# A graph network layer: three and two fetched sets of edges by turns instead of two, and two and one instead of one

## The chip, the cores and the metric

The kernel runs on one core of a Trainium2 chip. The metric is the device time of one execution in microseconds (us); lower is better.

## The reference

50,000 nodes with 160 features (64 scalars `s`, 32 vectors `v` of three) and 1,650,000 edges sorted by destination. Each edge brings the features of its source node, multiplied with four numbers of its own; the products are summed by destination, go through linear maps, and the result is added and normalised:

```python
ss, vv = (s[src], v[src])
e0 = sh[:, 0:1]; e1 = sh[:, 1:4]
dot = jnp.einsum('eui,ei->eu', vv, e1)
out0 = C0 * (ss * e0 @ W1 + dot * INV3 @ W2)
p3 = (ss @ W3)[:, :, None] * e1[:, None, :] * INV3
p4 = jnp.einsum('eui,uw->ewi', vv * e0[:, :, None], W4) * INV3
p5 = jnp.einsum('eui,uw->ewi', jnp.cross(vv, e1[:, None, :]), W5) * INV6
out1 = C1 * (p3 + p4 + p5)
m = jnp.concatenate([out0, out1.reshape(-1, 3 * MUL1)], axis=1)
m_agg = jax.ops.segment_sum(m, dst, num_segments=n)
...
return x + jax.nn.relu(h)          # h: m_agg through Ws and Wv
# outside: _layernorm(x + that, axis=-1)
```

## The kernel before

All maps are linear in the source's features, so the kernel sums first: for each destination it sums (four numbers of the edge) x (160 features of its source), and multiplies with one combined weight matrix afterwards.

Edges stand in sets of 128, called units in the code. Six sets make a group (`G`), whose destinations lie within 32 slots; two groups make a pair (`PG`), ten pairs (`per`) a chunk of 120 sets. For each set PE multiplies a 128x128 operand `ha` (slot times the four numbers, made by VectorE at L474 and L477 one pair ahead) with the 128x160 features of the sources (L502). After a pair VectorE transposes the sums (L518) and adds them into a ring of node sums in SBUF (L527). When 128 nodes are complete, `do_block` (PE, L822) multiplies with the weights, two such blocks at a time go through the normalisation (`norm1` on VectorE at L185 to L190, the root on ScalarE at L195, `norm3` on VectorE at L199 to L201), and SyncE sends the result (L920).

The features of the sources are the gathers. Most sets come by one indirect DMA that POOL issues (`gather`, L459) into `xg`, a pool of four buffers of a pair each, so POOL can be ahead of PE by up to four pairs. The others are fetched by ScalarE and SyncE (`Fetcher`, L351 to L391): for each of 128 edges the engine issues a DMA of one row of 640 bytes (L376) at an address from a register; 32 registers at a time are loaded from the list that VectorE made (`list_rows`, L403 and L404; load at L372). PE waits for the set's own semaphore. `deal` spreads the rows of a chunk evenly over ten pairs, from the fourth pair of the chunk before (`FBEGIN`) on; the place of a set in its chunk is chosen so that it is used four pairs (`FWAIT`) after its last row was issued. `BY_SCALAR` and `BY_SYNC` are the sets in a chunk; each pool has one buffer more. Fetching covers all chunks but the first two and the last.

SyncE's queue also issues all other transfers in program order. For a pair p: raw edge data of the chunk after next (`load`, L270 and L276, three pairs before a chunk begins); the residual rows `xt` of a pair of blocks (L765); the nodes' own rows and shares for the ring (`ask_own`, L798, five pairs before they are due, used by `set_own` at L807 two pairs before); the results.

Besides, the edges without self loops are packed. A "pack" takes 128 rows of 1,185 edges (SyncE reads them, L596 to L600), converts them on ScalarE (L604 to L606, L624), compacts them on VectorE (L625 to L690) and stores them row by row from SyncE into a table in DRAM (`store`, L739, two DMAs a row), which later chunks read instead of the raw edges. There are 11 packs; each pack's steps are spread over the pairs until it is due, its stores are 17 of them with one step between each two, and the next pack's conversion (L604) reuses the buffer that the stores read. Packs are due about every nine chunks; the first, which is needed soonest, has its stores within about one chunk.

All engines but POOL keep the order in which the program issues their work.

Of the kernel before, what the change touches and what calls it, by code (L numbers as in the profile page):

```python
# [39 lines left out]
F32 = mybir.dt.float32  # L40
I32 = mybir.dt.int32
# [3 lines left out]
ALU = mybir.AluOpType  # L45
AX = mybir.AxisListType
ET = mybir.EngineType
# [3 lines left out]
P = 128  # L51
MUL0, MUL1 = 64, 32
D = MUL0 + 3 * MUL1
# [10 lines left out]
W = 32  # L64
# [3 lines left out]
PG = 2  # L68
# [9 lines left out]
KM = WS - 1  # L78
REST = 15
LEAD = 3  # L80
BY_SCALAR, BY_SYNC = 2, 1
FBEGIN, FWAIT = 4, 4

def plan(n_nodes, n_edges):

    nblk = 125
    assert n_nodes % nblk == 0
    assert W == FB
    nb = n_nodes // nblk
    again = 9  # L90

    per_unit = P * n_nodes / n_edges
    group = max(g for g in range(1, 17)
                if g == 1 or (g + 0.2) * per_unit + 1 + 5 * math.sqrt(g * per_unit * per_unit / P) <= W)
    head = math.ceil(min(HEAD, n_edges / (group * P)) / SG) * SG
    eh = head * group * P
    row = group * P * 3 // 2 + math.floor(per_unit * group * 3 / 2 * (1 - n_nodes / n_edges))
    assert row * n_nodes / n_edges + 5 * math.sqrt(row * n_nodes / n_edges / 16) < KM

    far = math.ceil(6 * math.sqrt(n_edges) / 2 * n_nodes / n_edges) + 2  # L100
    rows = math.ceil((n_edges - eh) / row) + 2
# [7 lines left out]
def tile_gnn_resnorm(ctx: ExitStack, tc: tile.TileContext, x, src, dst, attr, W1, W2, W3, W4, W5, Ws, Wv, out, n_edges):  # L109
    nc = tc.nc  # L110
    N = x.shape[0]
    NBLK, NB, GA, G, NU, NG, L, NH, NR, FAR = plan(N, n_edges)
# [107 lines left out]
    NSC = math.ceil(NG / SG)  # L220
# [12 lines left out]
    with tc.tile_pool(name="once", bufs=1) as once, tc.tile_pool(name="raw", bufs=2) as rawp, \  # L233
# [8 lines left out]
        spotp, ownp, listp, heldp, scalarp, syncp = (  # L242
            later_pools.enter_context(tc.tile_pool(name=name, bufs=bufs))
            for name, bufs in (("spot", 3), ("own", 2), ("list", 2), ("held", 1),
                               ("scalar", BY_SCALAR + 1), ("sync", BY_SYNC + 1)))
        extremes = once.tile([P, 2, NSC], F32, name="extremes")
        count_ = once.tile([1, SG], F32, name="count")
        nc.gpsimd.iota(count_, pattern=[[1, SG]], base=0, channel_multiplier=0, allow_small_or_imprecise_dtypes=True)
# [8 lines left out]
        per = SG // PG  # L257
# [92 lines left out]

        class Fetcher:  # L351

            def __init__(self, engine, et, pool, n, place):
                self.engine, self.et, self.pool, self.n = engine, et, pool, n
                self.rows, self.turn, self.left, self.asked = deque(), 0, 0, []
                self.landed = [tc.alloc_semaphore(f"{pool.name}{i}") for i in range(4 * (n + 1))]
                self.spots = [math.ceil((FBEGIN + per * (i + 1) / n + FWAIT - per) * PG * G) + place for i in range(n)]
                assert all(0 <= at < per * PG * G for at in self.spots)

            def prepare(self, s, line, at, u):  # L360

# [19 lines left out]

                self.rows.extend(partial(one, q, e) for q in range(P // W) for e in range(W))

            def begin(self, wanted):
                assert len(self.rows) == wanted * self.n * P
                self.left = len(self.rows)

            def deal(self, gone):
                keep = math.floor(P * self.n * (1 - gone))
                while self.left > keep:  # L390
                    self.rows.popleft()()  # L391
                    self.left -= 1

        fetchers = [Fetcher(*f) for f in ((nc.scalar, ET.Activation, scalarp, BY_SCALAR, 2), (nc.sync, ET.SP, syncp, BY_SYNC, 8)) if f[3]]
        wanted = [(f, at) for f in fetchers for at in f.spots]
        assert len({at for _, at in wanted}) == len(wanted)

        def list_rows(s, u0, ef):

            line = listp.tile([P, len(wanted), W], I32, name="line")  # L400
            held = heldp.tile([P, len(wanted), W], F32, name="held")
            for i, (f, at) in enumerate(wanted):
                nc.vector.tensor_scalar(held[:, i], ef[:, 0, (u0 + at) % NK], 0.0, float(N - 1), op0=ALU.max, op1=ALU.min)  # L403
            nc.vector.tensor_scalar(line, held, float(4 * D), None, op0=ALU.mult)  # L404
            for i, (f, at) in enumerate(wanted):
                f.prepare(s, line[:, i], at, u0 + at)

# [436 lines left out]
        spots = once.tile([1, 2 * npacks * RP], I32, name="spots")  # L844
# [10 lines left out]
        counts = once.tile([P, 2, npacks], F32, name="counts")  # L855
# [9 lines left out]
        def after_pair(p, f, *args):  # L865
            later.setdefault(p, []).append((f, args))
# [135 lines left out]
        for p, (s, g, ng) in enumerate(pairs):  # L1002
            if (p + LEAD) % per == 0 and (p + LEAD) // per + 1 < NSC or not p:
                ahead_ = (p + LEAD) // per + 1
                end = reach(ahead_)
                assert end <= 0 or rows_stored[0] == NR or end <= row_start(rows_stored[0])[0][0]
                raws[ahead_] = load(ahead_)
            if p % per == 0 and s + 1 < NSC:
                after_pair(p + 1, do_cast, s + 1)
                after_pair(p + 2, do_place, s + 1)  # L1010
                if s + 2 == NSC:
                    after_pair(p + 4, examine_all)
                    after_pair(p + 6, read_flags)
            rows = gather(s, placed[s], (g - s * SG) * G, ng * G)
            for j, ps in enumerate(group_sums(p, rows, has.pop(p))):
                if j == 1 and turning:
                    turn_sums(*turning)
                    turning = None
                if j == 3 and p + 1 < len(pairs):
                    s1, g1, ng1 = pairs[p + 1]  # L1020
                    has[p + 1] = spread(placed[s1], (g1 - s1 * SG) * G, ng1 * G)
                work(1.0)
                if p % per == FBEGIN and not j:
                    begun_at = p
                    for f in fetchers:
                        f.begin(0 < s < NSC - 2)
                for f in fetchers:
                    if f.left:
                        f.deal((p - begun_at + (j + 1) / (ng * G)) / per)
                if packs and p >= START:  # L1030
                    when = p + (j + 1) / (ng * G)
                    todo = math.ceil(len(packs[0]) * min(1, (when - began) / max(1, due[0] - began)))
                    for step in packs[0][done:todo]:
                        if step:
                            step()
                    done = max(done, todo)
                    if done == len(packs[0]):
# [37 lines left out]
    with tc.tile_pool(name="up", bufs=1) as up, tc.tile_pool(name="us", bufs=2) as us, tc.For_i(0, once_more, 1):  # L1075
# [18 lines left out]
        for s in range(nseg):  # L1094
# [7 lines left out]
            for c in range(CB):  # L1102
# [3 lines left out]
                at = us.tile([PB, 2, SEG], F32, name="at")  # L1106
# [5 lines left out]
        f = up.tile([PB, CB], F32, name="f")  # L1112
# [12 lines left out]
    with tc.tile_pool(name="edges2", bufs=2) as ep, tc.tile_pool(name="ops2", bufs=2) as op, \  # L1125
            tc.tile_pool(name="node2", bufs=1) as np_, tc.tile_pool(name="psA2", bufs=2, space=PSUM) as psA, \
            tc.tile_pool(name="psF2", bufs=1, space=PSUM) as psF:
        with tc.For_i(0, blocks, 1) as b:
# [35 lines left out]
            for h in range(2):  # L1164
# [3 lines left out]
                at = np_.tile([D // 2, NK, NBLK], F32, name=f"ac{h}")  # L1168
# [3 lines left out]
            i = 0  # L1172
# [44 lines left out]
```

## Time and profile before

| | |
|---|---|
| Median of 3 runs | 15449.47 us (15443.1 to 15450.64) |
| Profiled execution | 15440.23 us, its span 15438.1 us |
| Granted TensorE clock, mean | 0.578 |
| Indirect gathers on POOL (L459) | 12,216 |
| Rows issued by ScalarE, by SyncE (L376) | 26,112 and 13,056 |

Rows of the profile name engine, line, operation and tiles; "x" is a count. A group's last columns are busy us, the mean ns of one, and the idle time before its instructions with what ended it; "issue" is time in which an engine waited for nothing that the profile shows. Rows of the view of waits read "who <- whom: us in total, times, longest us". Timeline rows are start and duration in us. ACTq and SPq are DMAs issued from ScalarE's and SyncE's queues; issuing is not counted as busy time. In the view of one line, three numbers with slashes are the shortest, median and longest duration in ns, followed by the first and last start in us.

### The profile page before, as it was taken

To read this page: it belongs to the slowest core of one execution; us is meant where nothing else is said; L and a number is where in the kernel's file an instruction comes from. 1 tells how busy PE (TensorE), PEld (TensorE's weight loads), DVE (VectorE), ACT (ScalarE), POOL (GpSimd) and SP (SyncE) were. 2 spreads that over 40 slices of the span, in tenths; PEclk is the share of its full clock that TensorE was granted. 3 is DMA by queue.
4 is the path that set the end of the run, shared out by engine and by line. 5 is a ranking of instruction groups with operands and counts; after the bars stand their busy time and mean duration, and the time that the engine had idled before them with its cause. 6 is when DMAs were issued, how large, how long until landed. Compare 5 with 4: busy or idle time off the path is not lost.

```text
span 15438.1 us, 175175 instructions
## 1 busy us (share of the span) xinstructions
PE 10171.0 (66%) x28971; PEld 6746.8 (44%) x28972; DVE 7652.8 (50%) x12634; ACT 171.5 (1%) x273; POOL 11585.0 (75%) x12229
## 2 busy tenths in 40 slices
PE   3466666666666666666666666666666666666666
PEld 3344444444444444444444444444444444444444
DVE  8465355435635553563455355435634553554333
ACT  0000000000000000000000000000000000000000
POOL 7677777777777777777777777777777777777777
PEclk6655555555555555555555555555555555555555
DMA  3333333333333333333333333333333333333332
GB/s 83 87 85 93 93 81 83 98 86 85 91 93 83 84 95 89 84 84 97 85 85 91 91 82 85 96 89 83 83 100 86 82 87 93 81 86 85 85 82 75
DMA packets 909328, 1346.94 MB, mean 87 GB/s; under 512 B 292862, under 2 KB 683298, under 8 KB 905526
## 3 DMA queue, kind: packets, MB, share of 16 engines
q0 software_dynamic: 586368, 1001.52, 25.4%
q1 hardware_dynamic: 268330, 316.48, 6.6%
q10 hardware_dynamic: 53488, 17.70, 0.6%
q14 instruction: 911, 7.46, 0.2%
q8 instruction: 231, 3.78, 0.1%
HBM read 1263.28 MB, written 71.42 MB: 86 GB/s over the span
## 4 chain that ended last, share of the span: by engine, by line
POOL 51%; issue 21%; DMA 19%; PE 4%; DVE 1%; SPq 0%; POOLq 0%; DVEq 0%
POOL xg L459 51%; DMA xg<-in_x,si 18%; PE ps L502 3%; DMA selves<-mine 1%; PE phb L822 0%; DVE ha L477 0%; SPq L739 0%; DVE prow L688 0%; DVE ring L527 0%; SPq L376 0%; DMA xt<-in_x 0%; DVE sums L518 0%; DVE hot L474 0%; DVE ring L813 0%; DVE xr L809 0%
## 5 line engine op out<-in xcount | busy, mean ns | idle before, releaser
L459 POOL DMA_INDIRECT xg<-in_x,si x12216 | 11581.5, 948 | 3831.6 <-issue 3491.8
L502 PE MATMUL ps<-xg,ha 128*128 128x160 f32 x24432 | 9418.3, 500 | 5253.2 <-DMA xg<-in_x,si 4659.5
L502 PEld LDWEIGHTS ps<-xg,ha 128*128 128x128 f32 x24432 | 5765.7, 292 | 8675.4 <-DMA xg<-in_x,si 7382.9
L518 DVE STREAM_TRANSPOSE sums<-ps 128x320 f32<-128x320 f32 x1044 | 536.1, 513 | 6766.0 <-PE ps L502 6736.7
L477 DVE TENSOR_TENSOR ha<-hot,pk 128x1536 f32<-128x1536 f32 x1044 | 1830.4, 1753 | 35.8
L822 PE MATMUL phb<-BWk,ring 128*128 128x160 f32 (+1 forms) x3910 | 1250.3, 417 | 0.0
L822 PEld LDWEIGHTS phb<-BWk,ring 128*128 128x128 f32 (+1 forms) x3910 | 1020.3, 294 | 0.0
L527 DVE TENSOR_TENSOR ring<-ring,sums 128x160 f32 x2087 | 684.5, 328 | 338.0 <-issue 202.3
L474 DVE TENSOR_TENSOR hot<-bank,rel 128x384 f32<-128x384 f32 x1044 | 573.1, 549 | 69.9 <-DMA xt<-in_x 68.1
L688 DVE COPY_PREDICATED prow<-marks,prow 128x2370 f32<-128x2370 int32 (+5 forms) x198 | 548.6, 2770 | 1.1
L813 DVE STREAM_TRANSPOSE ring<-xr 128x1280 f32<-128x1280 f32 x188 | 468.7, 2493 | 6.5
L688 DVE COPY_PREDICATED pra<-marks,pra 128x1580 f32<-128x1580 int32 (+5 forms) x198 | 377.1, 1905 | 0.0
L809 DVE TENSOR_TENSOR xr<-xr,bank 128x1280 f32<-128x1280 f32 x188 | 278.9, 1483 | 6.6 <-DVE bank L808 0.2
L185 DVE SCALAR_TENSOR_TENSOR y<-phb,xt 128x320 f32<-128x320 f32 x196 | 95.5, 487 | 256.7 <-PE phb L822 256.0
L195 ACT ACTIVATE rstd<-mv,eps_t 128x2 f32<-128x2 f32 x196 | 58.0, 296 | 14013.9 <-DVE mv L190 13216.5
L524 DVE TENSOR_TENSOR ring<-ring 128x196 f32<-128x196 f32 (+20 forms) x485 | 149.3, 374 | 1.8
L502 PE MATMUL ps<-xscalar,ha 128*128 128x160 f32 x408 | 146.9, 462 | 0.0
L201 DVE TENSOR_SCALAR o<-y,mv,rstd 128x160 f32<-128x160 f32 x391 | 130.8, 376 | 7.5
L685 DVE COPY_PREDICATED_SCALAR hit<-marks,none 128x395 int32 (+5 forms) x198 | 129.8, 655 | 7.0
L772 DVE MEMSET ring<- 128x1280 f32 (+1 forms) x98 | 119.3, 1218 | 22.6 <-issue 22.6
L189 DVE BATCH_NORM_STATS2 st<-y 128x6 f32<-128x160 f32 x391 | 121.6, 311 | 6.7
L686 DVE COPY_PREDICATED hit<-marks,pri 128x395 int32<-128x395 int32 (+5 forms) x198 | 118.2, 597 | 6.8
(353 smaller groups left out, 2187.4 us busy)
## 6 DMA issues: line engine op xcount, KB each, us to landing
xscalar<-in_x ACTq DMA_DIRECT2D x26112, 0.6 KB
xsync<-in_x SPq DMA_DIRECT2D x13056, 0.6 KB
xg<-in_x,si POOLq DMA_INDIRECT x12216
xr<-in_x SPq DMA_DIRECT2D x187, 640.0 KB
r<-edges SPq DMA_DIRECT2D x100, 384.0 KB
edges<-prow SPq DMA_DIRECT2D x1330, 27.8 KB
xt<-in_x SPq DMA_DIRECT2D x195, 160.0 KB
out<-o SPq DMA_DIRECT2D x195, 160.0 KB
```

Source lines behind the costliest of these rows:

```text
L201: nc.vector.tensor_scalar(o[:n, i], y[:n, i], mv[:n, i, 0:1], rstd[:n, i:i + 1], op0=ALU.subtract, op1=ALU.mult)
L459: nc.gpsimd.indirect_dma_start(out=xg[:, j, :], out_offset=None, in_=x, in_offset=bass.IndirectOffsetOnAxis(ap=placed[0][:, u + j:u + j + ...
L474: idle[:] = [nc.vector.tensor_tensor(hot[:, :n], slotsP[:, 0:W].unsqueeze(1).to_broadcast([P, n, W]), rel[:, u:u + n].unsqueeze(2).to_broa ...
L477: nc.vector.tensor_tensor(ha[:, :n], hot[:, :n].unsqueeze(2).to_broadcast([P, n, NK, W]), pk[:, :, u:u + n].rearrange("p k u -> p u k").un ...
L502: mm = nc.tensor.matmul(ps[:, j // G, :], ha[:, j].rearrange("p k w -> p (k w)"), xr, start=j % G == 0, stop=j % G == G - 1)
L518: nc.vector.transpose(at[:, :ng], ps[:, :ng].rearrange("p g (b f) -> p g b f", f=FB))
L524: nc.vector.tensor_tensor(ring[k][:, b, :past], ring[k][:, b, :past], ring[k - 1][:, b, S:S + past], op=ALU.add)
L527: nc.vector.tensor_tensor(here, here, at[:, i], op=ALU.add)
L688: nc.vector.copy_predicated(what[:n, a:e], mi[:, r].unsqueeze(2).to_broadcast([n, e - a, what.shape[2]]), what[:n, a + d:e + d])
L809: nc.vector.tensor_tensor(xr[:, :nq], xr[:, :nq], sumP[:, :nq].unsqueeze(2).to_broadcast([P, nq, D]), op=ALU.mult)
L813: nc.vector.transpose(ring[k][:, :, c0:c0 + nq * W].rearrange("p b (w q) -> p q b w", q=nq), xr[:, :nq].rearrange("p q (b f) -> p q b f", ...
L822: wrote("misc", nc.tensor.matmul(ph[:nb], ring[k][:, i, c0:c0 + nb], BWk[:, i, :], start=i == 0, stop=i == ND - 1))
```

## The change

The number of fetched sets becomes a function of the chunk. ScalarE fetches three sets for chunk 6, two for chunk 7, and so on by turns; SyncE two for chunk 8, one for chunk 9, and so on. Chunks 2 to 5 have no fetched set from ScalarE and chunks 2 to 7 none from SyncE. The places of the sets in a chunk follow from the count by the same rule as before, both pools have a buffer more, and a chunk with nothing to fetch makes no list.

```diff
-BY_SCALAR, BY_SYNC = 2, 1
+BY_SCALAR, SCALAR_FIRST = (3, 2), 6
+BY_SYNC, SYNC_FIRST = (2, 1), 8
...
-                               ("scalar", BY_SCALAR + 1), ("sync", BY_SYNC + 1)))
+                               ("scalar", max(BY_SCALAR) + 1), ("sync", max(BY_SYNC) + 1)))
...
-                self.spots = [math.ceil((FBEGIN + per * (i + 1) / n + FWAIT - per) * PG * G) + place for i in range(n)]
-                assert all(0 <= at < per * PG * G for at in self.spots)
+            def spots(self, s):
+                n = self.counts[s % len(self.counts)] if self.first <= s < NSC - 1 else 0
+                ats = [math.ceil((FBEGIN + per * (i + 1) / n + FWAIT - per) * PG * G) + self.place for i in range(n)]
+                assert all(0 <= at < per * PG * G for at in ats)
+                return ats
...
-            def begin(self, wanted):
-                assert len(self.rows) == wanted * self.n * P
-                self.left = len(self.rows)
+            def begin(self, s):
+                assert not self.left and len(self.rows) == len(self.spots(s + 1)) * P
+                self.all = self.left = len(self.rows)
...
-                keep = math.floor(P * self.n * (1 - gone))
+                keep = math.floor(self.all * (1 - gone))
...
+        MOST = max(BY_SCALAR) + max(BY_SYNC)
+        fetchers = [Fetcher(nc.scalar, ET.Activation, scalarp, BY_SCALAR, SCALAR_FIRST, 2),
+                    Fetcher(nc.sync, ET.SP, syncp, BY_SYNC, SYNC_FIRST, 8)]
...
+            wanted = [(f, at) for f in fetchers for at in f.spots(s)]
+            assert len({at for _, at in wanted}) == len(wanted)
+            if not wanted:
+                return
+            line = listp.tile([P, MOST, W], I32, name="line")
...
-                        f.begin(0 < s < NSC - 2)
+                        f.begin(s)
```

More of the change, by code (lines that the diff above doesn't have):

```diff
@@ L351, in tile_gnn_resnorm, with __init__ @@
         class Fetcher:
[L353 to L356, printed above, removed]
-                self.spots = [math.ceil((FBEGIN + per * (i + 1) / n + FWAIT - per) * PG * G) + place for i in range(n)]
-                assert all(0 <= at < per * PG * G for at in self.spots)
+            def __init__(self, engine, et, pool, counts, first, place):
+                self.engine, self.et, self.pool, self.counts, self.first, self.place = engine, et, pool, counts, first, place
+                self.rows, self.turn, self.all, self.left, self.asked = deque(), 0, 0, 0, []
+                self.landed = [tc.alloc_semaphore(f"{pool.name}{i}") for i in range(4 * (max(counts) + 1))]
+            def spots(self, s):
[3 more added lines that the diff above has]
+                return ats
             def prepare(self, s, line, at, u):
@@ L392, in deal @@
                     self.left -= 1
-        fetchers = [Fetcher(*f) for f in ((nc.scalar, ET.Activation, scalarp, BY_SCALAR, 2), (nc.sync, ET.SP, syncp, BY_SYNC, 8)) if f[3]]
-        wanted = [(f, at) for f in fetchers for at in f.spots]
-        assert len({at for _, at in wanted}) == len(wanted)
+        MOST = max(BY_SCALAR) + max(BY_SYNC)
+        fetchers = [Fetcher(nc.scalar, ET.Activation, scalarp, BY_SCALAR, SCALAR_FIRST, 2),
+                    Fetcher(nc.sync, ET.SP, syncp, BY_SYNC, SYNC_FIRST, 8)]
         def list_rows(s, u0, ef):
-            line = listp.tile([P, len(wanted), W], I32, name="line")
-            held = heldp.tile([P, len(wanted), W], F32, name="held")
+            wanted = [(f, at) for f in fetchers for at in f.spots(s)]
[3 more added lines that the diff above has]
+            line = listp.tile([P, MOST, W], I32, name="line")
+            held = heldp.tile([P, MOST, W], F32, name="held")
             for i, (f, at) in enumerate(wanted):
                 nc.vector.tensor_scalar(held[:, i], ef[:, 0, (u0 + at) % NK], 0.0, float(N - 1), op0=ALU.max, op1=ALU.min)
-            nc.vector.tensor_scalar(line, held, float(4 * D), None, op0=ALU.mult)
+            nc.vector.tensor_scalar(line[:, :len(wanted)], held[:, :len(wanted)], float(4 * D), None, op0=ALU.mult)
             for i, (f, at) in enumerate(wanted):
```

## The prediction

> **What bounds the kernel now.** I read the page first, then POOL's waits over the whole span and without its first 700 us, then the timeline of POOL.
>
> ```profile
> span 15438.1 us, 175175 instructions
> POOL 51%; issue 21%; DMA 19%; PE 4%; DVE 1%; SPq 0%; POOLq 0%; DVEq 0%
> L459 POOL DMA_INDIRECT xg<-in_x,si x12216 | 11581.5, 948 | 3831.6 <-issue 3491.8
> xscalar<-in_x ACTq DMA_DIRECT2D x26112, 0.6 KB
> xsync<-in_x SPq DMA_DIRECT2D x13056, 0.6 KB
> q0 software_dynamic: 586368, 1001.52, 25.4%
> q10 hardware_dynamic: 53488, 17.70, 0.6%
> ```
> ```profile
> POOL xg L459 <- issue: 3491.8, 11413, 2.0
> POOL xg L459 <- PE ps L502: 185.1, 437, 33.7
> ```
> ```profile
> POOL xg L459 <- PE ps L502: 133.2, 423, 1.1
> ```
> ```profile
> 8008.34 0.95 POOL L459 DMA_INDIRECT xg<-in_x,si  x1 [0.30 <-issue]
> 8009.60 0.95 POOL L459 DMA_INDIRECT xg<-in_x,si  x1 [0.30 <-issue]
> 8010.85 0.95 POOL L459 DMA_INDIRECT xg<-in_x,si  x1 [0.30 <-issue]
> ```
>
> POOL issues one gather of 128 edges after another: 0.95 us of work and 0.30 us before the next, a pitch of 1.25 us. 12,216 gathers at that pitch are 15,270 us of the 15,438. The chain says the same: POOL and issue hold 72%, and "DMA" on it is the landing of POOL's gathers. POOL almost never waits for anyone: the fourth view (waits from 700 us to 15,400 us) has no wait for PE over 1.1 us, the whole span has one of 33.7 us. So time is (number of gathers) x 1.25 us, plus what stalls POOL, and the only stall is in the first 700 us.
>
> The other sets of 128 edges, 26,112 / 128 = 204 and 13,056 / 128 = 102, come as single rows from ScalarE's and SyncE's queues. PE's matmuls are the same whichever way a set comes:
>
> ```profile
> PE 10171.0 (66%) x28971; PEld 6746.8 (44%) x28972; DVE 7652.8 (50%) x12634; ACT 171.5 (1%) x273; POOL 11585.0 (75%) x12229
> ```
>
> PE is busy 66% and DVE 50%, so neither takes POOL's place when POOL does one per cent less.
>
> **The change part by part.** *Fewer gathers.* There are 12,216 + 306 = 12,522 sets, 120 to a chunk, so 105 chunks (0 to 104); 2 to 103 are now served by the queues. After: ScalarE serves chunks 6 to 103, 49 with three sets and 49 with two, 245 sets; SyncE serves 8 to 103, 48 with two and 48 with one, 144 sets. Together 389 against 306, so 83 gathers leave POOL: 83 x 1.25 = 104 us. On the path, since POOL waits for nothing in the steady part.
>
> *ScalarE's issue time.* Its rows in two chunks of the middle:
>
> ```profile
> 7949.86 34.49 ACTq L376 DMA_DIRECT2D xscalar<-in_x  x90
> 8007.05 0.30 ACT L195 ACTIVATE rstd<-mv,eps_t 128x2 f32<-128x2 f32 x1 [87.63 <-DVE mv L190]
> 8007.12 65.88 ACTq L376 DMA_DIRECT2D xscalar<-in_x  x128
> 8082.40 0.29 ACT L195 ACTIVATE rstd<-mv,eps_t 128x2 f32<-128x2 f32 x1 [75.05 <-DVE mv L190]
> 8082.47 37.69 ACTq L376 DMA_DIRECT2D xscalar<-in_x  x90
> ```
>
> A row costs 34.49 / 90 = 0.38 to 37.69 / 90 = 0.42 us with the loading of its addresses; the 128 in 65.88 us hold a wait besides. Three sets are 384 x 0.40 = 154 us, two are 102 us. A chunk will last 115 to 117 gathers, 144 to 146 us. ScalarE falls some 10 us behind in a chunk of three and regains 44 us in one of two: 256 us of 290. Its rows have four pairs of groups (58 us) between the end of their issue and their use, and the normalisation's root (L195) waits for DVE today, so ScalarE comes to it early. I cost this at nothing; the cover is the 58 us for rows, and for the root the one pair (14.6 us) until VectorE uses it.
>
> *SyncE's issue time, in quiet chunks and while the row table is stored.* Quiet, and in a stretch in which a pack's rows are stored (L739):
>
> ```profile
> 8066.86 13.45 SPq L376 DMA_DIRECT2D xsync<-in_x  x33
> ```
> ```profile
> 8574.45 0.29 SPq L739 DMA_DIRECT2D edges<-prow  x1
> ...
> 8585.31 0.22 SPq L739 DMA_DIRECT2D selves<-mine  x1
> 8585.62 5.74 SPq L376 DMA_DIRECT2D xsync<-in_x  x18
> 8592.76 0.29 SPq L739 DMA_DIRECT2D edges<-prow  x1
> ```
>
> 13.45 / 33 = 0.41 us a row, so a second set costs 52 us of a chunk, and a quiet chunk with two sets takes 104 of 144 us. While a pack is stored, 16 stores take 11 us and with 18 rows and a load of addresses the round is 8592.76 - 8574.45 = 18.3 us. By the program a round falls in about every 1.3 pairs, some 19 us: SyncE is full there already. A second set in one of the two storing chunks puts SyncE 52 us later, and a further part of a set, some 15 us, before the last loads that hurt. What waits behind it: the node rows and shares for the ring (L798, used by VectorE at L807 three pairs later), the residual rows (L765), the raw edges (L276, L270), the results (L920).
>
> *What a late SyncE costs is read from the first pack*, whose stores are pressed into 250 us:
>
> ```profile
> POOL xg L459 <- PE ps L502: 48.3, 2, 33.7
> DVE hot L474 <- DMA xt<-in_x: 68.1, 1, 68.1
> PE ps L502 <- DVE ha L477: 58.1, 1, 58.1
> DVE hit L625 <- ACT marks L624: 47.2, 2, 36.7
> ACT prow L604 <- DMA edges<-prow: 142.6, 1, 142.6
> ```
>
> (waits from 560 to 720 us). VectorE waits 68.1 us for residual rows that SyncE issued late, PE then 58.1 us for its operand, POOL 48.3 - 33.7 = 14.6 us for a free buffer. So 68.1 - 14.6 = 53.5 us of lateness are swallowed by the four row buffers. Right after, ScalarE is held until the stores have landed (142.6 us), VectorE waits 36.7 us for ScalarE, and POOL pays 33.7 us, nearly all of it, as PE had not caught up.
>
> *Later packs.* The worst of them in the trace, waits from 1300 to 2000 us:
>
> ```profile
> DVE sa L807 <- DMA sa<-selves: 20.3, 3, 13.3
> POOL xg L459 <- PE ps L502: 5.5, 18, 0.3
> ```
> ```profile
> DVE sa L807 <- DMA sa<-selves: 30.6, 6, 13.3
> ```
>
> A wait of 13.3 us cost POOL nothing. With 52 + 15 us more it is 80 us, of which 80 - 53.5 = 27 us would reach POOL. In the eight other full packs such waits are 30.6 - 20.3 = 10.3 us over three times (the second view is the whole span); even all of it in one place and 52 us more are 62 us, 9 us for POOL. Upper bound 27 + 8 x 9 = 99 us, lower bound nothing, as part of the 11 us that 16 stores take is waiting for DMA, which rows between them can use. I take 10 us, near the lower end, since the only long stall in the trace needed 68 us.
>
> *The first pack without rows.* No set is fetched for chunks 2 to 5 by ScalarE nor for 2 to 7 by SyncE. In the stores of the first pack SyncE issued these rows:
>
> ```profile
> L376 SPq DMA_DIRECT2D xsync<-in_x x101: 225/229/1186, 409.2 to 656.3; - x101
> L739 SPq DMA_DIRECT2D edges<-prow x136: 223/228/1047, 412.2 to 662.5; - x136
> ```
>
> (408 to 663 us). 101 x 0.41 = 41 us go, so the stores end near 622 us and not 663, and POOL, with about five more gathers by then, comes there 6 us later. Lateness before was 48.3 + 53.5 = 102 us; now 102 - 41 - 6 = 55 us, about what the buffers swallow. Of 48 us stall I take 45 us gone, bounds 20 (only the first wait and a little) and 48. Next late there is nothing that the view shows: ScalarE's rows, held behind L604, are gone too.
>
> *Lists.* 83 more list instructions on VectorE, which idles half the time: nothing.
>
> *DMA engines.* q10 (ScalarE's) holds 0.6% of 16 engines for 26,112 rows, 0.006 x 16 x 15438 / 26112 = 0.06 us a row; q0 25.4%, 5.1 us a gather. 83 sets add 83 x 128 x 0.06 = 640 engine-us and remove 425: no change. The Trainium skill ("DMA: Bandwidth & Descriptors", Bandwidth, Measured) speaks against the trade: it wants transfers of 1 MiB and calls those under 64 KB dominated by their descriptors, and these have 0.6 KB. By that rule the extra rows would be paid for somewhere; the rows above show that the price falls on the two issuing queues, which had room, and no run yet shows it with more rows.
>
> Sum: -104 - 45 + 10 = -139 us. The profiled execution took 15,440.2 us (span 15,438.1 and 2.1 around it), 9.2 us under the median of 15,449.5 of the three runs. 15,449.5 - 139 = 15,310 us, 0.9% less.
>
> **The rivals.** *The first stall stays* (chance 0.13): the stores of the first pack are limited by their DMAs, not by SyncE, so they end at 663 us anyhow. For it: waits for DMA among the stores. Against: 101 rows stood between them. Then -104 + 10 = -94, or 15,355 us, and up to 15,444 at the upper bound of the storing packs.
>
> *SyncE becomes the bound while packs are stored* (0.09). Point of decision: VectorE's wait at L807 or L185 beyond 53.5 us in each of the nine later full packs. If each costs POOL what the first did, 48 us, 9 x 48 = 432 us are lost against 149 gained: 15,449.5 + 283 = 15,733 us, slower. For it: the full round of 18.3 us. Against: the later packs are stored over two chunks and only one of them gets a second set.
>
> *The pitch grows* (0.04): with more single rows in flight POOL's descriptors take longer. One per cent of 1.25 us on 12,133 gathers is 152 us, and no gain is left: 15,310 + 152 = 15,462 us. This is where the Trainium skill's rule on small transfers would show. Against: the pitch above, 1.25 us, was read while ScalarE issued its 128 rows from 8007.12 us on.
>
> **How the numbers follow.** The forecast has 0.74. Its own range is -104 - 48 = -152 to -104 - 20 + 99 = -25 us, 15,297 to 15,424 us, and the runs before spread by 8 us (15,443 to 15,451): 15,289 to 15,425 us, with the first rival's 15,355 inside, holds nearly all of 0.74 + 0.13; the other two are left out. Over 0.2% (31 us, about what a measurement of this kernel can tell from no change) faster: 0.74 + 0.13 = 0.87; within: 0.04; slower: 0.09.
>
> **What would show it.** Right: 12,133 gathers at a pitch of 1.25 us; POOL's wait for PE before 700 us gone; the stores of the first pack ended near 620 us; ScalarE's idle time before L195 shorter, VectorE's waits at L807 up to 60 us while POOL's longest wait stays under some 20 us. Wrong: POOL waits for PE of tens of us in chunks in which a pack is stored, VectorE waiting for ScalarE at L199, or a longer pitch.

## The result: 1.8% slower

The changed kernel took 15,720.44 us (median of 4 runs, 15,707.07 to 15,724.42), the kernel before 15,449.07 us (4 runs, 15,443.1 to 15,450.64): a ratio of 1.0177, 95% interval 1.0164 to 1.0189. The forecast was 15,310 us, with a range up to 15,425 us. The changed kernel is slower, so the forecast was wrong in its sign.

The lines of the page of the changed kernel (lines of the program have moved by up to nine: the gathers are now L468, PE's matmul of them L511, VectorE's use of the nodes' own shares L816, SyncE's stores L748):

```profile
span 15722.4 us, 196747 instructions
...
q0 software_dynamic: 582384, 994.71, 27.7%
...
q10 hardware_dynamic: 63984, 21.08, 0.8%
...
L468 POOL DMA_INDIRECT xg<-in_x,si x12133 | 11505.7, 948 | 4188.6 <-issue 3332.9
```

There are 83 gathers fewer, 12,133, and each still takes 948 ns. What grew is POOL's idle time before its gathers, from 3,831.6 to 4,188.6 us. The view of waits says in front of what (who waits for whom: us, times, longest us). One line of the kernel before that the prediction did not show, then the kernel after:

```profile
POOL xg L459 <- DMA xg<-in_x,si: 140.4, 328, 1.7
```
```profile
POOL xg L468 <- issue: 3332.9, 10802, 2.3
...
DVE sa L816 <- DMA sa<-selves: 936.9, 46, 77.8
...
POOL xg L468 <- DMA xg<-in_x,si: 589.6, 952, 4.5
...
DVE hit L634 <- ACT marks L633: 439.4, 26, 43.1
...
PE ps L511 <- DMA xsync<-in_x: 295.3, 17, 42.9
...
POOL xg L468 <- PE ps L511: 248.9, 333, 26.8
```

The same view for SyncE's queue, before and after:

```profile
SPq L739 <- DMA edges<-prow: 618.4, 511, 7.1
```
```profile
SPq L748 <- DMA edges<-prow: 880.9, 616, 12.6
```

POOL waits for landings of its own gathers 952 times instead of 328; each such wait holds the 0.30 us that stand before a gather anyway, so 589.6 - 952 x 0.30 = 304 us are lost there, against 140.4 - 328 x 0.30 = 42 us before. And it waits for PE up to 26.8 us, with VectorE waiting up to 77.8 us for the nodes' own shares, which SyncE's queue brings late. PE also waits, 17 times and up to 42.9 us, for the sets that SyncE fetches itself; the kernel before has no such wait.

From the start times of all gathers in the two traces I split the time as follows. The undisturbed pitch of a gather is 1.251 us; a pause of 0.02 to 2 us more than that is called small, one over 2 us a stall:

| us | before | after | change |
|---|---|---|---|
| gathers x 1.251 | 15,282 | 15,178 | -104 |
| small pauses (count) | 89.9 (466) | 343.4 (1,058) | +253 |
| stalls before 700 us | 47.7 (2) | 0 | -48 |
| stalls after 700 us | 0 | 177.5 (23) | +177 |
| rest | 18 | 23 | +5 |
| span | 15,438.1 | 15,722.4 | +284 |

The saving is there, as the undisturbed pitch is the same in both traces, and the stall of the first pack has gone. Two losses, 430 us together, stand against that. The larger one, the small pauses, is the one that the prediction priced at nothing.

**What a small pause is.** The timelines of POOL and of PE in the kernel after, in a stretch of small pauses (3950 to 3975 us; start us, duration us, in brackets the idle time before and what ended it):

```profile
3964.81 0.94 POOL L468 DMA_INDIRECT xg<-in_x,si  x1 [0.49 <-DMA xg<-in_x,si]
3966.61 0.94 POOL L468 DMA_INDIRECT xg<-in_x,si  x1 [0.85 <-DMA xg<-in_x,si]
3968.02 0.95 POOL L468 DMA_INDIRECT xg<-in_x,si  x1 [0.47 <-DMA xg<-in_x,si]
3969.50 0.94 POOL L468 DMA_INDIRECT xg<-in_x,si  x1 [0.53 <-DMA xg<-in_x,si]
```
```profile
3964.60 0.90 PE L511 MATMUL ps<-xg,ha 128*128 128x160 f32 x2 [0.23 <-DMA xg<-in_x,si]
3966.39 0.90 PE L511 MATMUL ps<-xg,ha 128*128 128x160 f32 x2 [0.89 <-DMA xg<-in_x,si]
3967.81 0.90 PE L511 MATMUL ps<-xg,ha 128*128 128x160 f32 x2 [0.51 <-DMA xg<-in_x,si]
3969.28 4.82 PE L511 MATMUL ps<-xg,ha 128*128 128x160 f32 x12 [0.58 <-DMA xg<-in_x,si]
```

Each gather of POOL starts 0.2 us after PE has begun a set: 3964.60 and 3964.81, 3966.39 and 3966.61, and so on. One landing releases both. It isn't the same set: counted over the trace, 256 of the 343 us of small pauses fall on gathers that start when PE has six or seven of the gathers issued still to begin. So PE begins one gather, and POOL then issues the one seven or eight places further on. The reason is in the semaphores that the trace names: the gathers' completions count on eight of them used in turn, and a gather is issued only when the one eight places before it, the last that used its semaphore, has landed wholly. At a pitch of 1.25 us a landing may take up to about 10 us before that costs anything. Over the gathers for which the trace holds all completions, 1.3% took longer than 10 us before, and 10.7% after (median 4.5 us before, 6.8 us after). Of the small pauses for which it holds them too (305 us), 192 us end within 0.4 us after the last completion of the gather eight before.

**Which landings are late.** A gather writes 16 completions. Most come 1.75 to 2.75 us after its issue. I counted, 2.85 us after the issue of each gather, how many completions of it and of all gathers before it were still missing. Before, four to six were missing at 1,475 gathers of 12,216; after, at 3,409 of 12,133. At the small pauses five are missing, with the two gathers issued last not counted yet: about one completion of each gather still open. So 15 of the 16 shares are in time, and one runs several gathers behind. The trace shows it directly: in the kernel after the 15th completion comes at a median of 2.6 us after the issue and the 16th at 6.8 us; in the kernel before it is 2.5 and 4.5 us.

Within the trace of the kernel after, the 16th completion also goes with the single rows in flight. Its median is 2.6 us where no row was issued in the 10 us before the gather, 5.9 us with 17 to 24 rows and 8.3 us with more than 40, while that of the 15th stays at 2.6 us.

### The profile page after: what moved, and what is told of

Read it like the earlier page. It is cut to its first block, busy times and chain, and to the rows that moved or that the text cites. A ratio compares the mean times of both kernels' runs of the same rounds, so it can differ in the third digit from the quotient of the medians.

```text
span 15722.4 us, 196747 instructions
## 1 busy us (share of the span) xinstructions
PE 9548.4 (61%) x28971; PEld 6555.6 (42%) x28972; DVE 7659.1 (49%) x12713; ACT 171.3 (1%) x273; POOL 11509.2 (73%) x12146
## 3 DMA queue, kind: packets, MB, share of 16 engines
q0 software_dynamic: 582384, 994.71, 27.7%
q10 hardware_dynamic: 63984, 21.08, 0.8%
## 5 line engine op out<-in xcount | busy, mean ns | idle before, releaser
L468 POOL DMA_INDIRECT xg<-in_x,si x12133 | 11505.7, 948 | 4188.6 <-issue 3332.9
L511 PE MATMUL ps<-xg,ha 128*128 128x160 f32 x24266 | 8785.9, 483 | 5862.8 <-DMA xg<-in_x,si 4161.2
L511 PEld LDWEIGHTS ps<-xg,ha 128*128 128x128 f32 x24266 | 5571.4, 285 | 8847.5 <-DMA xg<-in_x,si 6520.3
L816 DVE TENSOR_TENSOR sa<-sa,bank 128x32 f32<-128x32 f32 x188 | 30.3, 161 | 936.9 <-DMA sa<-selves 936.9
L511 PE MATMUL ps<-xsync,ha 128*128 128x160 f32 x288 | 92.8, 417 | 295.3 <-DMA xsync<-in_x 295.3
L511 PEld LDWEIGHTS ps<-xsync,ha 128*128 128x128 f32 x288 | 70.3, 279 | 301.1 <-DMA xsync<-in_x 301.1
L511 PE MATMUL ps<-xscalar,ha 128*128 128x160 f32 x490 | 166.4, 439 | 0.0
```

Of the source, the lines that this page charges most:

```text
L468: nc.gpsimd.indirect_dma_start(out=xg[:, j, :], out_offset=None, in_=x, in_offset=bass.IndirectOffsetOnAxis(ap=placed[0][:, u + j:u + j + ...
L511: mm = nc.tensor.matmul(ps[:, j // G, :], ha[:, j].rearrange("p k w -> p (k w)"), xr, start=j % G == 0, stop=j % G == G - 1)
```

## The experiments

The kernel before has two times. In some sets of runs it takes about 15,450 us, as above; in others about 21,000 us, where ScalarE's rows cost twice as much and ScalarE is the bound. One and the same chip gave both, and I do not know what sets it. Experiments are compared within their own set only; those in the slower sets come last.

### The two parts alone, and without the storing packs

`f_late` has the old counts but the new first chunks; `f_scalar` and `f_sync` have one engine's new counts each; `f_quiet` is the changed kernel with one set for SyncE in the 18 chunks of two whose rows are issued while a pack is stored.

```diff
# f_late
+BY_SCALAR, SCALAR_FIRST = (2,), 6
+BY_SYNC, SYNC_FIRST = (1,), 8
# f_scalar
+BY_SCALAR, SCALAR_FIRST = (3, 2), 6
+BY_SYNC, SYNC_FIRST = (1,), 8
# f_sync
+BY_SCALAR, SCALAR_FIRST = (2,), 6
+BY_SYNC, SYNC_FIRST = (2, 1), 8
# f_quiet, beside the whole change
+STORING = {9, 11, 19, 27, 29, 37, 39, 47, 49, 57, 65, 67, 75, 77, 85, 87, 95, 97}
...
+                if self.engine is nc.sync and s - 1 in STORING:
+                    n = min(n, 1)
```

> The later start alone once more (two sets on ScalarE from chunk 6, one on SyncE from chunk 8, 12,230 gathers), for a chip on which the kernel before takes 15,449 us. Both theories: the first stall of 48 us goes, 14 gathers more are 17.5 us, 15,419 us. Where the kernel before takes 21,200 us instead, ScalarE's rows bind and the ratio is that of the first try, 0.992.

> ScalarE's three and two sets alone (SyncE one set from chunk 8, 12,181 gathers). Theory A (SyncE late while packs are stored costs): 15,357 us. Theory B (more single rows in flight slow the landing of the gathers and POOL's pitch): about 15,480 us, POOL's pauses of 0.02 to 2 us near 200 us in all. Theory C, new from the first tries (the price of a row on its issuing queue decides, ScalarE's queue is full): slower than 15,449 with VectorE waiting for ScalarE at L200.

> SyncE's two and one sets alone (ScalarE two sets from chunk 6, 12,182 gathers). Theory A: about 15,700 us, the long waits of VectorE at the node shares (sa) as in the changed kernel, 900 us. Theory B: about 15,660 us with pauses of POOL in quiet chunks too. Theory C: as A, since SyncE's queue is the one that is full while packs are stored.

> The changed kernel, but SyncE fetches one set and not two in the 18 two-set chunks whose fetching falls together with stores of a pack, 12,151 gathers. Theory A: the loss is gone, 65 gathers less than before and no first stall, 15,449 - 81 - 48 = 15,320 us. Theory B: the small pauses in the other chunks stay, about 170 us more than before, 15,490 us. Theory C: ScalarE's full queue still costs, between the two.

The kernel before took 15,442.68 us beside them. "Missing" is the number of gathers at which four to six completions were missing, as above.

| | us | ratio (95%) | gathers | small pauses, us | stalls, us | missing |
|---|---|---|---|---|---|---|
| before | 15,442.68 | | 12,216 | 90 | 48 | 1,475 |
| f_late | 15,404.27 | 0.9976 (0.9966 to 0.9986) | 12,230 | 88 | 4 | 1,287 |
| f_sync | 15,393.04 | 0.9968 (0.9957 to 0.9979) | 12,182 | 98 | 18 | 1,629 |
| f_scalar | 15,438.92 | 0.9998 (0.9988 to 1.0008) | 12,181 | 163 | 12 | 2,238 |
| f_quiet | 15,497.24 | 1.0030 (1.0019 to 1.0040) | 12,151 | 259 | 13 | 2,864 |
| after (its own set) | 15,720.44 | 1.0177 (1.0164 to 1.0189) | 12,133 | 343 | 178 | 3,409 |

The waits of `f_sync`, then of `f_quiet`:

```profile
DVE sa L816 <- DMA sa<-selves: 683.7, 36, 49.2
...
POOL xg L468 <- DMA xg<-in_x,si: 162.9, 369, 2.6
...
POOL xg L468 <- PE ps L511: 129.9, 375, 13.8
```
```profile
POOL xg L471 <- DMA xg<-in_x,si: 423.7, 749, 2.9
...
DVE sa L819 <- DMA sa<-selves: 272.4, 24, 42.7
...
POOL xg L471 <- PE ps L514: 114.3, 361, 2.1
```

Theories A and B of these expectations both missed `f_sync` (15,393 us against 15,700 and 15,660), and B was 40 us too high for `f_scalar` and 7 us off for `f_quiet`. Four things follow. Without the first stall the kernel gains 38 us, though POOL has 14 gathers more (`f_late`). SyncE's second set alone is a gain: VectorE waits 684 us for what SyncE brings late, but never over 49.2 us at once, and POOL pays 18 us; late SyncE alone does not make the loss. ScalarE's third set alone eats its own saving: 35 gathers fewer than before, and 73 us more of small pauses. And without SyncE's lateness in storing packs the changed kernel is still slower than before: no wait of POOL for PE is over 2.1 us, but 259 us of small pauses remain. Each row of the table with more completions missing has more pauses; neither part alone comes near to what both do together. The number of rows is not all of it: `f_scalar` and `f_sync` have about as many (43,648 and 43,520), and ScalarE's cost more. Why is open.

### Four sets in each chunk instead of five and three

```diff
-BY_SYNC, SYNC_FIRST = (2, 1), 8
+BY_SYNC, SYNC_FIRST = (1, 2), 8
```

> The changed kernel with SyncE's counts turned round (one set in even chunks, two in odd ones): four fetched sets in every chunk instead of five and three by turns, and as many gathers to within one. If what costs is the coincidence of ScalarE's third and SyncE's second set (the late DMA engine's backlog builds in chunks of five), small pauses fall from 343 us to 150 to 250 us and the time to 15,550 to 15,630 us. If only the number of rows in the whole run counts, the time stays at about 15,700 us.

Measured: 15,636.17 us beside 15,473.13 us of the kernel before, ratio 1.0104 (1.0087 to 1.0121), which is 15,610 us on the scale of 15,449. Small pauses 237 us, stalls 167 us, 2,740 gathers with completions missing.

```profile
DVE sa L816 <- DMA sa<-selves: 997.2, 47, 76.4
...
POOL xg L468 <- DMA xg<-in_x,si: 391.8, 706, 3.7
...
POOL xg L468 <- PE ps L511: 268.4, 327, 27.8
```

As many rows and gathers as in the changed kernel, spread more evenly, and 106 us less of small pauses. So part of it is the coincidence of the two extra sets, as the first theory of this experiment says; the stalls stay, as it says too.

### A semaphore for each gather

```diff
+        gathers, landed = [], [tc.alloc_semaphore(f"gathered{i}") for i in range(4 * PG * G)]
...
+                    turn = len(gathers)
+                    sem, count, key = landed[turn % len(landed)], 16 * (turn // len(landed) + 1), f"gather{turn}"
+                    rows[j] = xg[:, j, :], sem, count, key
+                    got = nc.gpsimd.indirect_dma_start(
...
+                    got.then_inc(sem, 16)
+                    tc.no_tile_sem_insts.add(got.ins.name)
+                    tc.add_to_no_dep_group(key, got.ins)
+                    gathers.append(got)
```

48 semaphores are as many as the four buffers of a pair have sets, so POOL waits for no landing any more, only for PE to free a buffer.

> The changed kernel, but each gather counts on a semaphore of its own out of 48 (PE waits for it as it does for fetched sets) instead of on one of eight used in turn. Theory D: POOL's small pauses come 0.2 us after PE has started the gather eight before, so POOL waits until the gather eight before has landed wholly; of the 16 completions of a gather 15 are in time and one DMA engine's is up to six gathers late, the engine that carries the single rows. On a chip where the kernel before takes 15,440 us D expects POOL's small pauses to fall from 343 us to under 100 us and the time to about 15,720 - 250 = 15,470 us, less if the stalls behind late SyncE (177 us) are swallowed better as well. Theory E (the pauses are made in POOL or in making its descriptors): no change, 15,690 to 15,750 us. If the late engine is simply full, POOL's pauses become waits for PE and the time stays at 15,700 us.

Measured: 15,589.25 us beside 15,473.13 us, ratio 1.0077 (1.006 to 1.0094), 1.0% less than the changed kernel's ratio. POOL's waits:

```profile
PE ps L519 <- DMA xg<-in_x,si: 3892.9, 5622, 6.2
POOL xg L472 <- issue: 3593.1, 11780, 0.3
...
DVE sa L824 <- DMA sa<-selves: 1152.5, 51, 84.5
...
POOL xg L472 <- PE ps L519: 436.9, 317, 51.6
```

The row of POOL's waits for its own landings is gone; small pauses are 40 us instead of 343. At 3,479 gathers completions are missing, as many as in the changed kernel: the shares land as late as before, and POOL no longer minds. This shows that the wait for the gather eight before makes the small pauses. The time did not fall by 250 us as expected, but by some 150: stalls rose from 178 to 339 us, as VectorE now waits up to 84.5 us for SyncE. I take it that POOL's pauses had given SyncE time to come nearer; that was not tried by itself.

### Each row in four pieces

The tiles of fetched sets get a gap of 16 bytes after every 160, so that the four pieces of a row can't be joined; PE reads them across the gaps.

```diff
-                        tile_.append(self.pool.tile([P, D], F32, name="x" + self.pool.name))
+                        tile_.append(self.pool.tile([P, 4, D // 4 + 4], F32, name="x" + self.pool.name))
...
+                    row = self.engine.dma_start(tile_[0].bitcast(U8)[p:p + 1, :, :D],
+                                                xbytes[ds(self.asked[e], 4 * D)].rearrange("(o c f) -> o c f", o=1, c=4))
```

> The changed kernel, but the tiles of fetched sets have a gap of 16 bytes after every 160, so that each single row is moved as four pieces of 160 bytes in one DMA instead of one piece of 640. Theory D: if the four pieces go to four DMA engines, three or four completions of a gather are late instead of one; if bytes are what costs, each is less late, small pauses fall from 343 us towards 100 us and the time to about 15,500 us; if the number of pieces is what costs, the time is 15,720 us or more. If all four pieces stay on one engine it is later than before and the time well over 15,720 us. Theory E: no change. Rows might also cost more to issue; then ScalarE and SyncE are late and POOL waits for PE.

Measured: 26,377.47 us, ratio 1.7047 (1.7018 to 1.7075). The page, the waits and ScalarE's timeline:

```profile
q10 hardware_dynamic: 252144, 21.45, 0.9%
```
```profile
DVE rstd L200 <- ACT rstd L196: 15141.5, 173, 146.9
POOL xg L468 <- PE ps L512: 11191.5, 369, 113.7
...
POOL xg L468 <- DMA xg<-in_x,si: 25.3, 80, 1.0
```
```profile
8192.89 107.24 ACTq L381 DMA_DIRECT2D xscalar<-in_x  x131
```

Packets of ScalarE's queue rose from 63,984 to 252,144, from two a row (640 bytes and a completion) to eight, four pieces and four completions. A row costs 107.24 / 131 = 0.82 us to issue instead of 0.40, and ScalarE is the bound. POOL is held by PE and hardly waits for its landings any more (25.3 us): the experiment does not tell which DMA engine the rows load, and that stays open.

The Trainium skill ("DMA: Bandwidth & Descriptors", "Why a DMA increments its semaphore by 16 and not by 1") says that a DMA issued from ScalarE's or SyncE's queue which uses only k of the 16 engines uses the lowest-numbered k, and that a gather has landed only with all 16 completions. The trace agrees as far as it goes: one data packet and one completion a row, four of each with four pieces, and one share of a gather late, the more so the more rows were issued just before. That the late share is the one of the rows' engine fits, but the trace does not name engines, so it is not shown.

### Both causes away

`f_quiet`'s change and a semaphore for each gather together.

> The changed kernel with SyncE at one set in the 18 two-set chunks that fall into a pack's stores (12,151 gathers), and a semaphore of its own for each gather out of 48. On the ordinary chip the first of the two alone took 15,497 us, 1.003 of the kernel before, with 259 us of small pauses and 13 us of stalls. If the wait for the gather eight before and SyncE's lateness in storing packs are the whole loss (theory D with A), small pauses fall to about 40 us, stalls stay under 40 us, and the time is about 0.99 of the kernel before, 15,280 us. If the one late DMA engine is full, the pauses come back as waits of POOL for PE and the ratio stays at 1.000 to 1.004. On a chip where single rows are slow to issue ScalarE binds and neither shows.

Measured: 15,277.06 us (4 runs, 15,273.88 to 15,277.8) beside 15,451.53 us of the kernel before: ratio 0.9888 (0.9871 to 0.9904). It beats both kernels. Its page and waits:

```profile
span 15272.1 us, 190699 instructions
...
L475 POOL DMA_INDIRECT xg<-in_x,si x12151 | 11530.8, 949 | 3711.5 <-issue 3601.8
```
```profile
POOL xg L475 <- issue: 3601.8, 11805, 0.3
...
PE ps L522 <- DVE ha L497: 625.4, 65, 46.1
DVE sa L827 <- DMA sa<-selves: 417.2, 29, 42.9
...
POOL xg L475 <- PE ps L522: 98.4, 317, 1.9
```

Of POOL's 3,711.5 us of idle time 3,601.8 are the pitch. No stall is left, small pauses are 40 us, and at 3,185 gathers completions are missing without harm. Against the kernel before: 65 gathers x 1.251 = 81, small pauses 90 - 40 = 50, the first stall 48, in sum 179 us; the spans differ by 15,438.1 - 15,272.1 = 166. With the two causes away the prediction's gain is there, so they are the whole loss but for some 13 us. Of the gain, the 50 us of pauses are a loss that the kernel before had too.

### The sets in which ScalarE is the bound

Ten kernels ran where the kernel before takes 20,975 to 21,244 us. The first four:

> The kernel before, unchanged, profiled beside the next three so that its gather landings can be read from the same chip. Both theories: about 15,449 us, 12,216 gathers, one stall of POOL of some 48 us before 700 us, POOL's pauses of 0.02 to 2 us beyond its 1.25 us pitch about 80 us in all, and the mean packet of the gather's queue about 107 ns.

> Only the later start: two sets on ScalarE from chunk 6 and one on SyncE from chunk 8, 12,230 gathers. Theory A (SyncE late while packs are stored is what costs) and theory B (more single rows in flight slow the landing of POOL's gathers and so its pitch) agree: 14 gathers more are +17.5 us and the first stall of 48 us goes, 15,419 us. If the first stall's removal is worth nothing, 15,467 us.

> ScalarE's part alone: three and two sets from chunk 6, SyncE one set from chunk 8, 12,181 gathers. Theory A: SyncE is not later than before, so -35 gathers are -44 us and the first stall -48 us: about 15,357 us, no wait of VectorE at the node shares (sa) over 20 us. Theory B: 128 more rows in every second chunk lengthen the pitch, about half of the 250 us that small pauses of POOL gained: -92 + 125, about 15,480 us.

> SyncE's part alone: two and one sets from chunk 8, ScalarE two from chunk 6, 12,182 gathers. Theory A: all of the loss is here, -34 gathers are -43 us, the first stall -48 us, and the stalls of the storing packs and what follows them +350 us: about 15,700 us. Theory B: half of the small pauses and the large stalls of the storing packs (+125 and +177 us): about 15,660 us, with small pauses in quiet chunks too.

The kernel before there (`c_before`, one run, 21,176 us): its waits, and ScalarE's timeline.

```profile
DVE rstd L199 <- ACT rstd L195: 6863.3, 145, 79.0
POOL xg L459 <- PE ps L502: 4558.7, 367, 57.9
```
```profile
8115.51 108.83 ACTq L376 DMA_DIRECT2D xscalar<-in_x  x128
```

A row costs 108.83 / 128 = 0.85 us in this stretch, and 0.80 us over the whole run (26,112 rows in 20,803 us), so two sets a chunk take 204 us or more, longer than the chunk's gathers; VectorE waits for the root behind the rows (L199), and POOL for PE. Not every row is dearer: 64% of the rows still follow the one before them within 0.4 us, against 88% in the run at 15,450 us. But at 16% of the rows the register move that stands beside the DMA takes some 0.70 us. In the run at 15,450 us none takes over 0.04 us (shortest, median and longest in ns):

```profile
L376 ACTq MOVE xscalar<-in_x x26112: 29/29/38, 244.7 to 15251.2; - x200
```

So in these sets ScalarE's instructions themselves are held now and then, not the DMAs alone. The four pieces are another case: there most rows are dearer, with a median of 0.68 us from one to the next against 0.32. Ratios to the kernel before: `e_late` 0.9923 (0.9897 to 0.9948), `e_scalar` 1.104 (1.1001 to 1.1079), `e_sync` 1.0413 (1.0384 to 1.0442). Where rows cost that much, ScalarE's third set costs over 10%.

Later runs that fell into such sets could not tell what they were made for. `h_sems` and `h_even` are the programs of `i_sems` and `i_even`, `j_quiet_sems` that of `k_quiet_sems`; their ratios were 1.1044 (1.0999 to 1.109), 1.1152 (1.1087 to 1.1216) and 1.1112 (1.107 to 1.1153), all bound by ScalarE. The remaining three:

```diff
# h_four: four pieces without a gap, in both operands of the row's DMA
+ tile_[0].bitcast(U8)[p:p + 1].rearrange("o (c f) -> o c f", c=4)
# h_sems_sync: f_sync with a semaphore for each gather
# j_before_sems: the kernel before with a semaphore for each gather
```

> The changed kernel, but each single row is moved as four pieces of 160 bytes in one DMA instead of one piece of 640. Theory D (the engine that carries the single rows is late): if the pieces go to four DMA engines and their bytes are what costs, the late completions shrink, small pauses fall from 343 us towards 100 us and the time to about 15,500 us; if the number of pieces is what costs, four engines are late instead of one and the time is 15,720 us or more. Theory E (pauses made in POOL): no change. The price of issuing a row on its queue (0.33 us) could rise, which would show as a slower kernel with ScalarE or SyncE late, not with POOL waiting for its landings.

> ScalarE two sets throughout and SyncE two and one by turns, with the first rows at chunks 6 and 8 (15,393 us on this kind of chip), with a semaphore of its own for each gather. Theory D: POOL's small pauses (98 us) fall below 40 us, 15,393 - 60 = about 15,335 us. Theory E: 15,393 us. A candidate to beat both kernels.

> The kernel before with a semaphore of its own for each gather out of 48, nothing else changed: 12,216 gathers, 90 us of small pauses, 48 us of stall in the first pack. Theory D: small pauses fall to 30 to 40 us and the time to 15,443 - 55 = about 15,390 us. If the price of a semaphore of its own (more waits on PE) is felt, the time rises.

`h_four`, 1.1087 (1.1028 to 1.1146), still moved each row as one piece of 640 bytes, since the pieces lie side by side: it is the changed kernel over again, and led to `i_pad`. `h_sems_sync` had 1.0372 (1.0326 to 1.0418), about as `e_sync`. `j_before_sems` had 0.9997 (0.9972 to 1.0022): semaphores alone change nothing where ScalarE binds. What they give the kernel before at 15,450 us was not measured; of its small pauses they could save 90 us at most, so it would still be slower than `k_quiet_sems` by some 80 us, unless something else changed.

## Why the prediction was wrong

*Fewer gathers, -104 us: right*, as the account by start times shows. *The first stall, -45 us: right*, and the rival in which it stays is out. In the prediction's window (560 to 720 us) POOL's longest wait for PE is now 0.3 us, and the stores of the first pack end at 597 us, 25 us before the 622 forecast:

```profile
POOL xg L468 <- PE ps L511: 1.8, 6, 0.3
```
```profile
L748 SPq DMA_DIRECT2D edges<-prow x136: 223/228/805, 406.8 to 597.1; - x136
```

*ScalarE's issue time: right in the price.* In the kernel after a row costs 93.90 / 231 = 0.41 us, against 0.40 forecast:

```profile
8060.37 93.90 ACTq L381 DMA_DIRECT2D xscalar<-in_x  x231
```

*Storing packs, +10 us with an upper bound of 99: the mechanism right, the size wrong.* The stalls measure 177 us. Two places in the pack for which the prediction had 80 us (waits from 1600 to 1800 us, and from 1850 to 1960 us):

```profile
DVE sa L816 <- DMA sa<-selves: 72.4, 2, 68.8
...
POOL xg L468 <- PE ps L511: 18.0, 5, 15.5
```
```profile
PE ps L511 <- DVE ha L486: 69.4, 1, 69.4
DVE sa L816 <- DMA sa<-selves: 60.9, 2, 59.2
POOL xg L468 <- PE ps L511: 27.1, 2, 26.8
```

From VectorE's wait to POOL's the buffers swallow 68.8 - 15.5 = 53.3 and 59.2 - 26.8 = 32.4 us: the 53.5 us that the prediction took from the first pack hold in one place and are too kind in the other. VectorE's longest wait, 77.8 us, is in a later pack (at some 10,400 us), for which the prediction had 62 us at most. In the trace POOL has seven stalls over 10 us, of 10.7 to 26.5 us, 132 us together, in six packs, while they are stored or within 80 us after, from 1,700 to 13,500 us, and 45 us in 16 smaller ones. So what failed is, first, that one pack alone was given such a wait, and that 53.5 us were taken to be swallowed everywhere. Second, a wait was left out: SyncE's own fetched sets come late as well. Until 18 and 21 us before the stalls of 19.9 us (at 6,216 us) and 21.3 us (at 13,452 us) PE had waited 38.6 and 34.5 us for them; how much of the 177 us this makes is open. Third, the two edits were costed one by one, and ScalarE's third set slows SyncE's stores: their waits for landings are 618 us before and 654 us in `f_sync`, but 851 us in `f_scalar` and 881 us after. With SyncE's second set alone (`f_sync`) the term is nearly right: VectorE waits 49.2 us at most, and stalls are 18 us. That the slower stores lift this to 77.8 us fits, but was not tried by itself.

VectorE's 439 us of waits for ScalarE (L633), 76 us before, stand in front of none of the seven stalls over 10 us.

*DMA engines, "no change": the step that failed.* The prediction weighed the rows' busy time as a mean over 16 engines. That mean tells nothing here: q0 goes from 25.4% to 27.7%, but it has 28.0% in `f_late`, which pauses no more than the kernel before. A gather is not done with 15 of its 16 shares, and the eight semaphores turn one late share into a pause of POOL. Missing completions went from 1,475 to 3,409 gathers, small pauses from 90 to 343 us. Nearest to this is the rival "the pitch grows", with a chance of 0.04 and 152 us; the loss came to 253 us. Its cause, more single rows in flight, was right, but not its place: POOL's work on a gather stays at 948 ns, and what is late is the landing. What the prediction set against that rival was a row of three gathers in a quiet moment. Such rows are there after the change as well (around 8,000 us all are at 1.25 us), as the pauses come in runs. And the sign was there before the change: that POOL waits for nothing in the steady part left out its 328 waits for its own landings, 42 us of loss.

The Trainium skill's rule on small transfers ("DMA: Bandwidth & Descriptors", Bandwidth, Measured) pointed the right way: the rows were paid for, though by the landing of others and not by themselves.

*SyncE becomes the bound while packs are stored* was the rival at 15,733 us, next to the measured 15,720. The nearness is chance: it gave 432 us to stalls, which are 177, and nothing to pauses, which are 253.

## What to carry to other kernels

Where one engine issues transfers back to back and waits for completions that share few semaphores, ask how late the slowest share of a transfer may be before the issuer is held, and count the shares that are late: a mean over DMA engines doesn't show it. A saving that hands work to other queues should be checked for what those queues' transfers do to the landings of the ones that bind, and a slack (here 32 to 53 us of buffers, eight semaphores) should be compared with the sum of all edits that draw on it, as two edits that are harmless alone can pass it together. If the issuer is held by a semaphore and not by a buffer, more semaphores may be worth more than fewer transfers: here they gave the changed kernel 1.0%, where 83 gathers are worth 0.7%, and with SyncE spared while packs are stored they made a 1.8% loss into a 1.1% gain.

## What the hardware showed that was not expected

The price of issuing a single row is not fixed. It is 0.40 us in the runs at 15,450 us and 0.80 us in the sets where the same program took 21,000 us, where even a register move on ScalarE takes 0.70 us at one row in six; what sets this is open. It is 0.82 us where the row has four pieces and four completions. And one of a gather's 16 shares can run several gathers behind the other 15 (16th completion at a median of 6.8 us against 2.6 us for the 15th, one in ten later than 10 us), without POOL's own work (948 ns a gather) or its pitch in quiet moments showing anything of it.
